# The mean row of the last three tiles as products with their rows, and the expert scores ahead of their transposes

## The chip, the cores and the metric

The kernel runs on one core of one Trainium2 chip. The time is what the device takes for one execution, in microseconds (us). The kernel before took 1511.21 us, the median of three runs (1510.18 to 1511.75).

## The reference, cut to what matters

A graph of 1250 nodes with 512 features passes two layers. In the first, `x` becomes the sum of `x`, a graph convolution and an attention block with its own MLP. Then comes the step that the change is about, a mixture of 16 experts that sees all nodes as one sequence and so chooses one expert for all of them:

```python
scores = softmax(mean(u, axis=1) @ Wg + bg, axis=-1)   # u: layer norm of x, 1 x 1250 x 512
idx    = argmax(scores, axis=-1)
gate   = take_along_axis(scores, idx[:, None], axis=-1)
y      = einsum('bsd,bdo->bso', u, We[idx]) + be[idx][:, None, :]
x      = x + gate[:, :, None] * y
```

So the mean of all 1250 normalized rows is needed before the index, and the index before any byte of the chosen expert's weights (512 x 512) is fetched. The second layer (another graph convolution, an attention and eight experts of 2048 hidden features, two per node) follows.

## The kernel before, in words

The 1250 rows are ten tiles (`T`) of 125 (`P`); features are four chunks (`DC`) of 128. `xs[:, t, :]` holds the rows of tile t, rows on partitions. The program is unrolled Python. A framework takes the order of the instructions on each engine from a simulated run: an instruction of a later line goes ahead of an earlier one on the same engine when its inputs are there first. Each engine then carries out its own list in that order, and semaphores hold an instruction until what it needs is done. TensorE, VectorE, ScalarE, GpSimd and SyncE (which issues most transfers) each have such a list.

The end of the first layer's MLP works in three blocks of tiles, `blocks = ((0, 4), (4, 7), (7, T))` (L697). For each block, `mlp_hidden` and `mlp_out` make the rows (L710, L722), and `expert_rows(b)` (L733) follows one block later, for the last block directly after its `mlp_out` (L779). `expert_rows` does, for its tiles:

- mean and variance of each row into `mvf` (`stats`, L143), then 1/std into `rstd` (`inv_std`, L135: an add on VectorE, a square root on ScalarE, a reciprocal on VectorE). In the last block, `load_table` (L749) has ScalarE load the table of Exp.
- for each tile: the normalized rows `un` (L743, VectorE; two buffers, tag "row"), four transposes on TensorE into one PSUM buffer `pt` (`transposed`, L128 to L133; two buffers), a copy of `pt` to `ut[t]` on ScalarE (L746), and the sum of `pt` over its 125 rows into `sums_t[:, t, :]` on VectorE (L747).

The next phase (from L831) opens its own pools. VectorE adds the ten parts of `sums_t` (L835) and multiplies by 1/N (L836). TensorE multiplies the mean with the router's weights into `psc`, 1 x 16 (L839). Then come, on VectorE but for the Exp on ScalarE: the bias (L841), the maximum (L843), the difference (L844), Exp (L845), the sum (L846), its reciprocal (L847), the quotient (L848), the largest value (L850) and its index `best_i` (L852). SyncE loads the index into a register (L853) and issues the four pieces of the chosen expert's weights `we_sb` (L856), the bias `be_sb` (L858) and, behind them, six weights of the second layer (L862). TensorE spreads the gate over the partitions (L871) and multiplies `ut` with `we_sb`, 40 products (L893): the first four tiles together, the others one by one. L877 sets `b2_full` to zero on VectorE, for a later use.

Two helpers of other places serve as rows of comparison: `degrees` (L573) has products with a moving operand of one column, and `project` (L123) in the second layer's router has them eight columns wide. L1306 and L1329 are the products of the eight experts at the end, and L1366, L1399 and L1400 their branches, since how many rows an expert gets is known only on the chip.

## Time and profile before

| what | value |
| --- | --- |
| median of three runs | 1511.21 us |
| the profiled execution, its own time | 1508.84 us |
| its span, from first to last instruction | 1507.1 us |
| mean granted clock of TensorE | 0.966 of full |
| stretch 505.0 to 525.0: TensorE, VectorE, ScalarE busy | 8.33, 12.27, 7.76 us |
| the same stretch: granted clock | 0.74 |
| stretch 525.0 to 562.5: TensorE, VectorE busy | 37.21, 28.20 us |
| the same stretch: granted clock | 0.91 |
| L747, sum of a transposed tile | ten of 0.674 us (median) |
| L132 for `un`, a transpose | 40 of 0.270 us (median) |
| L746, copy of a transposed tile | 0.53 us each |
| L852, index of the best expert, ends | 520.96 us |
| L856, first weight transfer issued | 522.39 us |
| L893, first product with the expert's weights | 525.29 us |

Times within the execution count from the start of the span. In lists in order of time, the first number is the start, the second the time over which the merged instructions reach, then the engine (PE is TensorE, PEld its weight loads, DVE VectorE, ACT ScalarE, SPq the transfers that SyncE issues), the line, the operation, output and inputs, how many; in brackets stands the idle time before and what ended it. Lines of the form `A:B` give, for the stretch from A to B: its length, TensorE's busy time (instructions), the granted clock as a share of full, the share of the transfer engines and GB/s. Where a line gives durations as a/b/c, they are the least, the median and the largest in ns.

### The profile page before, as it was taken

The page shows a single profiled execution, that of the slowest core. Times are in us where ns is not written, and L with a number is a line of the kernel's source. Part 1 is how long each engine was busy: PE and PEld are TensorE (multiplying, and loading weights), DVE is VectorE, ACT ScalarE, POOL GpSimd, SP SyncE. Part 2 cuts the span into 40 slices and gives each one's busy share as a digit, 9 for nine tenths or more (in the row PEclk, how much of TensorE's full clock was granted, in tenths as well). Part 3 has the DMA queues.
Part 4 walks back from the last instruction along what each step waited for, and adds up shares of the span by engine and source line. Part 5 has one row for each costly group of instructions (what it writes and reads, how often), then busy time and mean ns, then how long its engine had stood idle before and what let it go on. Part 6 is the DMA issues. An engine that isn't in the chain of part 4 may idle for free. (4 is left out here: it accounts for less than half of the span.)

```text
span 1507.1 us, 18469 instructions
## 1 busy us (share of the span) xinstructions
PE 1392.5 (92%) x6082; PEld 871.0 (58%) x6082; DVE 586.0 (39%) x1425; ACT 404.9 (27%) x937; POOL 199.3 (13%) x176
## 2 busy tenths in 40 slices
PE   5999999999999699999965899899999999999997
PEld 3444445434554346554544697794767577975673
DVE  8887777699775673344476000000000000000000
ACT  8655445301223413112223221210212012110110
POOL 3345445400000000000005000000000000000000
PEclk9999999999999899999986999899999999999999
DMA  7312111522510030001149466600643006101011
GB/s 225 99 55 62 56 55 49 178 83 89 172 48 14 31 131 3 0 1 36 47 152 349 149 222 236 227 9 11 230 125 115 13 3 215 36 6 14 1 14 15
DMA packets 72766, 134.75 MB, mean 89 GB/s; under 512 B 8328, under 2 KB 9720, under 8 KB 72622
## 3 DMA queue, kind: packets, MB, share of 16 engines
q1 hardware_dynamic: 67694, 122.47, 24.0%
q0 software_dynamic: 4928, 10.43, 3.5%
q8 instruction: 82, 1.34, 0.4%
q14 instruction: 62, 0.51, 0.1%
HBM read 107.27 MB, written 26.38 MB: 89 GB/s over the span
## 5 line engine op out<-in xcount | busy, mean ns | idle before, releaser
L1329 PE MATMUL po<-w,big 128*128 128x512 f32 x576 | 250.1, 592 | 0.0
L1306 PE MATMUL pm<-hts,big 128*128 x960 | 183.3, 353 | 14.8 <-issue 13.5
L1318 DVE TENSOR_SCALAR o<-po,to_gate 128x512 f32<-128x512 f32 (+1 forms) x24 | 17.7, 749 | 452.9 <-PE po L1331 451.6
L1306 PEld LDWEIGHTS pm<-hts,big 128*128 128x128 f32 x960 | 165.8, 194 | 34.4 <-issue 19.0
L1329 PEld LDWEIGHTS po<-w,big 128*128 128x128 f32 x576 | 109.1, 190 | 132.1 <-issue 131.5
L1309 ACT ACTIVATE big<-pm,cols_sb 128x256 f32<-128x256 f32 (+2 forms) x224 | 96.2, 433 | 282.5 <-PE pm L1306 281.8
L1306 PE MATMUL pm<-hts,w 128*128 x832 | 143.5, 334 | 13.8 <-PEq L1399 5.9
L1306 PEld LDWEIGHTS pm<-hts,w 128*128 128x128 f32 x832 | 132.1, 197 | 24.6 <-issue 15.6
L455 PE MATMUL pm<-big,ht 128*125 128x512 f32 x240 | 130.9, 633 | 0.0
L1319 POOL DMA_INDIRECT out_dram<-o,row x24 | 37.0, 1540 | 645.2 <-DVE o L1318 284.2
L429 DVE TENSOR_TENSOR at<-at,pa 128x160 f32 x320 | 102.2, 319 | 41.3 <-PE pa L427 17.7
L400 POOL TENSOR_TENSOR hm<-hm,w_low 125x640 bf16<-125x640 bf16 x80 | 100.4, 1276 | 114.0 <-DVE hm L394 63.3
L123 PE MATMUL pm<-w,at 128*125 128x512 f32 x240 | 114.2, 598 | 0.0
L397 ACT ACTIVATE hm<-hm,w_top 125x80 bf16<-125x80 bf16 x320 | 86.4, 350 | 68.1 <-DVE hm L394 55.1
L633 PE MATMUL pn<-big,at 125*125 125x512 f32 x200 | 89.5, 605 | 3.0 <-DMA big<-q_d 3.0
L455 PE MATMUL pm<-big,xt 128*125 128x512 f32 x160 | 88.8, 646 | 1.2 <-DMA x_t<-in_x_dram 1.2
L1309 ACT ACT_TABLE_LOAD x11 | 14.1, 1283 | 248.9 <-PE pm L1306 248.9
L427 PEld LDWEIGHTS <-hs 125*128 125x128 bf16 x640 | 50.8, 97 | 48.8 <-issue 44.0
L424 PE MATMUL pa<-hm,hs 125*128 125x160 bf16 x320 | 64.6, 233 | 13.0 <-DVE at L429 10.9
L424 PEld LDWEIGHTS <-hs 125*128 125x128 bf16 x320 | 31.1, 97 | 67.8 <-issue 38.6
L633 PEld LDWEIGHTS pn<-big,at 125*125 125x125 f32 x200 | 37.5, 190 | 52.7 <-issue 52.7
L427 PE MATMUL pa<-hm,hs 125*128 125x80 bf16 x640 | 64.4, 198 | 0.0
(391 smaller groups left out, 1622.2 us busy)
## 6 DMA issues: line engine op xcount, KB each, us to landing
w<-in_w_dram SPq DMA_DIRECT2D x52, 1024.0 KB
big<-in_w_dram SPq DMA_DIRECT2D x12, 1024.0 KB
x_t<-in_x_dram SPq DMA_DIRECT2D x10, 224.0 KB
xn_d<-xr SPq DMA_DIRECT2D x10, 224.0 KB
y_d<-o SPq DMA_DIRECT2D x10, 224.0 KB
z_d<-o SPq DMA_DIRECT2D x10, 224.0 KB
q_d<-o SPq DMA_DIRECT2D x10, 224.0 KB
k_d<-o SPq DMA_DIRECT2D x10, 224.0 KB
```

Source lines behind the costliest of these rows:

```text
L123: nc.tensor.matmul(ps, lhs[:, c, :], w[:, c, :], start=(c == 0), stop=(row is None and c == DC - 1))
L397: nc.scalar.activation(hm[:, j, 1, :], hm[:, j, 0, :], AF.Copy, scale=w_top[:, g * J + j:g * J + j + 1])
L400: nc.gpsimd.tensor_tensor(hm[:, :, 2 + i, :], hm[:, :, 0, :], w_low[:, i, c8, None].to_broadcast([CH, J, TW]), ALU.mult)
L424: nc.tensor.matmul(pa.rearrange("p k c -> p (k c)"), hs[:, j, :], hm[:, j, 0:2, :].rearrange("p k c -> p (k c)"), start=True, stop=False)
L427: nc.tensor.matmul(pa[:, 1, :], hs[:, j, :], hm[:, j, 2 + i, :], start=False, stop=(i == 1))
L429: add = nc.vector.tensor_tensor(to, to, pa.rearrange("p k (t w) -> p k t w", t=T), ALU.add)
L455: nc.tensor.matmul(pm, lhs[:, c, :], w_sb[:, c, :], start=(c == 0), stop=(row is None and c == DC - 1))
L633: nc.tensor.matmul(pn, at[:P, 0, s, t * P:(t + 1) * P], y[:, s, :], start=(s == 0), stop=(s == T - 1))
L1306: nc.tensor.matmul(pm[:, :width], w1s[e, f // DC][:, c, (f % DC) * 128:(f % DC + 1) * 128], hts[:, c, bass.ds(start, width)], start=(c == ...
L1309: nc.scalar.activation(hid[f][:, :width], pm[:, :width], AF.Gelu, bias=cols_sb[:, C_B11 + e * FC + f:C_B11 + e * FC + f + 1])
L1319: nc.gpsimd.indirect_dma_start(out, bass.IndirectOffsetOnAxis(ap=row[:n], axis=0), o[:n], None, bounds_check=N - 1, oob_is_err=False, comp ...
L1329: nc.tensor.matmul(pm, hid[f][:, s * 128:(s + 1) * 128], w2s[e, f // DC][:, f % DC, :], start=(f == 0), stop=False)
```

## The change

In the last block (tiles 7, 8 and 9) the sum of the normalized rows is no longer taken from the transposes. The sum over rows of (x - mean) * rstd is the product of x with the column rstd, less the product of the row means with rstd. So TensorE takes, per tile, each 128-feature chunk of `xs` as the stationary operand and `rstd` as a moving operand of one column; a fifth column of `pmean` has the row means, spread over 128 columns, as the stationary operand. That is fifteen products. VectorE adds the seven earlier tiles' parts ahead of the block's statistics, copies the fifth column out, and updates the mean's sum with the other four. The scaling by 1/N moves into the step that adds the bias. The scores' chain, up to the index, moves from the next phase into `expert_rows`, behind the transposes of tile 7 and the scaled rows of tile 8 and ahead of the rest of tiles 8 and 9. `mean_t`, the scalars and the scores use space of `sums_t` and `bg_sb`; `best` and `best_i` move to a pool that lasts longer. The other two blocks work as before.

```diff
+    mean_t, spare = sums_t[:, T - 1, :], sums_t[:, T - 2, :]
...
         def expert_rows(b):
             first, last = blocks[b]
+            final = b + 1 == len(blocks)
+            if final:
+                nc.vector.tensor_reduce(mean_t, sums_t[:, :first, :].rearrange("p t c -> p c t"), AX.X, ALU.add)
             for t in range(first, last):
                 stats(mvf, t, xs[:, t, :])
             rstd = inv_std(mvf[:, first:last, 1], [P, last - first], "rstd2")
-            if b + 1 == len(blocks):
+            if final:
                 load_table(AF.Exp, rstd[0:1, 0:1])
-            for t in range(first, last):
-                un = mx.tile([P, D], F32, name="un", tag="row")
-                nc.vector.tensor_scalar(un, xs[:, t, :], mvf[:, t, 0:1], rstd[:, t - first:t - first + 1],
+                pmean = pa.tile([128, DC + 1], F32, name="pmean", tag="pa")
+                for c in range(DC + 1):
+                    for t in range(first, last):
+                        lhs = (xs[:, t, c * 128:(c + 1) * 128] if c < DC else
+                               mvf[:, t, 0:1].to_broadcast([P, 128]))
+                        nc.tensor.matmul(pmean[:, c:c + 1], lhs, rstd[:, t - first:t - first + 1],
+                                         start=(t == first), stop=(t == last - 1))
+            uns = {}
+            def un_of(t):
+                uns[t] = mx.tile([P, D], F32, name="un", tag="row")
+                nc.vector.tensor_scalar(uns[t], xs[:, t, :], mvf[:, t, 0:1], rstd[:, t - first:t - first + 1],
                                         op0=ALU.subtract, op1=ALU.mult)
-                pt = transposed(ps, un)
+            def turned_of(t):
+                pt = transposed(ps, uns[t])
                 nc.scalar.copy(ut[t], pt)
-                nc.vector.tensor_reduce(sums_t[:, t, :], pt, AX.X, ALU.add)
+                return pt
+            if not final:
+                for t in range(first, last):
+                    un_of(t)
+                    nc.vector.tensor_reduce(sums_t[:, t, :], turned_of(t), AX.X, ALU.add)
+                return
+            un_of(first)
+            turned_of(first)
+            un_of(first + 1)
+            less, one, score = spare[:, 0:1], spare[0:1, 1:2], bg_sb
+            nc.vector.tensor_copy(less, pmean[:, DC:])
+            nc.vector.scalar_tensor_tensor(mean_t, pmean[:, :DC], less, mean_t, op0=ALU.subtract, op1=ALU.add)
+            psc = pa.tile([1, E0], F32, name="psc", tag="pa")
+            for c in range(DC):
+                nc.tensor.matmul(psc, mean_t[:, c:c + 1], wg_sb[:, c, :], start=(c == 0), stop=(c == DC - 1))
+            nc.vector.scalar_tensor_tensor(score, psc, 1.0 / N, bg_sb, op0=ALU.mult, op1=ALU.add)
...
+            nc.scalar.activation(score, score, AF.Exp)
...
+            nc.vector.max(best, score)
+            nc.vector.max_index(best_i, best, score)
+            turned_of(first + 1)
+            for t in range(first + 2, last):
+                un_of(t)
+                turned_of(t)
...
-        mean_t = fp.tile([128, DC], F32, name="mean_t")
-        nc.vector.tensor_reduce(mean_t, sums_t.rearrange("p t c -> p c t"), AX.X, ALU.add)
-        nc.vector.tensor_scalar(mean_t, mean_t, 1.0 / N, None, op0=ALU.mult)
-        psc = pa.tile([1, E0], F32, name="psc", tag="pa")
...
-        nc.vector.max_index(best_i, best, score)
         chosen = nc.sync.value_load(best_i[0:1, 0:1], min_val=0, max_val=E0 - 1)
```

The lines left out between the scores and the index are the same steps in the same order as before.

More of the change, by code (lines that the diff above doesn't have):

```diff
@@ L537, in gps_two_layer_kernel @@
     sums_t = keep.tile([128, T, DC], F32, name="sums_t")
+    mean_t, spare = sums_t[:, T - 1, :], sums_t[:, T - 2, :]
+    best = keep.tile([1, 8], F32, name="best")
+    best_i = keep.tile([1, 8], U32, name="best_i")
     spots = [(t, D) for t in range(4)] + [(6, D), (7, D), (8, 0), (9, 0), (0, 0), (1, 0)]
@@ new lines, in expert_rows @@
+            psc = pa.tile([1, E0], F32, name="psc", tag="pa")
+            for c in range(DC):
+                nc.tensor.matmul(psc, mean_t[:, c:c + 1], wg_sb[:, c, :], start=(c == 0), stop=(c == DC - 1))
+            nc.vector.scalar_tensor_tensor(score, psc, 1.0 / N, bg_sb, op0=ALU.mult, op1=ALU.add)
+            nc.vector.tensor_reduce(one, score, AX.X, ALU.max)
+            nc.vector.tensor_scalar(score, score, one, None, op0=ALU.subtract)
+            nc.scalar.activation(score, score, AF.Exp)
@@ L749, in load_table @@
+            nc.vector.tensor_reduce(one, score, AX.X, ALU.add)
+            nc.vector.reciprocal(one, one)
+            nc.vector.tensor_scalar(score, score, one, None, op0=ALU.mult)
+            nc.vector.max(best, score)
[4 more added lines that the diff above has]
+                turned_of(t)
         def load_table(func, behind):
@@ L833, in gps_two_layer_kernel @@
             tc.tile_pool(name="fpa", bufs=1, space=PSUM) as pa:
-        mean_t = fp.tile([128, DC], F32, name="mean_t")
-        nc.vector.tensor_reduce(mean_t, sums_t.rearrange("p t c -> p c t"), AX.X, ALU.add)
-        nc.vector.tensor_scalar(mean_t, mean_t, 1.0 / N, None, op0=ALU.mult)
-        psc = pa.tile([1, E0], F32, name="psc", tag="pa")
-        for c in range(DC):
-            nc.tensor.matmul(psc, mean_t[:, c:c + 1], wg_sb[:, c, :], start=(c == 0), stop=(c == DC - 1))
-        score = fp.tile([1, E0], F32, name="score")
-        nc.vector.tensor_add(score, psc, bg_sb)
-        one = fp.tile([1, 1], F32, name="one")
-        nc.vector.tensor_reduce(one, score, AX.X, ALU.max)
-        nc.vector.tensor_scalar(score, score, one, None, op0=ALU.subtract)
-        nc.scalar.activation(score, score, AF.Exp)
-        nc.vector.tensor_reduce(one, score, AX.X, ALU.add)
-        nc.vector.reciprocal(one, one)
-        nc.vector.tensor_scalar(score, score, one, None, op0=ALU.mult)
-        best = fp.tile([1, 8], F32, name="best")
-        nc.vector.max(best, score)
-        best_i = fp.tile([1, 8], U32, name="best_i")
-        nc.vector.max_index(best_i, best, score)
         chosen = nc.sync.value_load(best_i[0:1, 0:1], min_val=0, max_val=E0 - 1)
```

## The prediction

> **What bounds the kernel now.** I read the page first: TensorE is busy 92% of the span, and section 2 shows its digits at 9 almost everywhere but in slices 13 and 14 (about 505 to 525 us). The chain of waits reaches back only into the last experts, so for the changed place I read the list of instructions in order of time, then stretches with the granted clock.

> ```profile
> PE 1392.5 (92%) x6082; PEld 871.0 (58%) x6082; DVE 586.0 (39%) x1425; ACT 404.9 (27%) x937; POOL 199.3 (13%) x176
> ```

> ```profile
> 512.49 0.18 DVE L140 RECIPROCAL rstd<-rstd 125x3 f32<-125x3 f32 x1 [0.27 <-ACT rstd L139]
> 513.40 1.07 PE L132 MATMUL pt<-ident,un 125*128 125x125 f32 x8 [3.16 <-DVE un L743]
> 515.49 1.06 PE L132 MATMUL pt<-ident,un 125*128 125x125 f32 x4 [1.01 <-DVE sums_t L747]
> 516.72 0.48 DVE L877 MEMSET b_full<- 96x512 f32 x1 [0.80 <-PE pt L132]
> 517.20 0.68 DVE L747 TENSOR_REDUCE sums_t<-pt 128x4 f32<-128x500 f32 x1
> 517.91 0.22 DVE L835 TENSOR_REDUCE mean_t<-sums_t 128x4 f32<-128x40 f32 x1
> 518.51 0.27 PEld L839 LDWEIGHTS psc<-w,mean_t 128*1 128x1 f32 x8 [2.35 <-issue]
> 519.65 0.21 ACT L845 ACTIVATE score<-score 1x16 f32<-1x16 f32 x1 [2.48 <-DVE score L844]
> 525.29 0.50 PEld L893 LDWEIGHTS pm<-we_sb,at 128*125 128x125 f32 x2 [4.05 <-DMA we_sb<-in_we_dram]
> ```

> The reader is to see one serial chain in which TensorE mostly idles: 1/std of the last tiles (ready 512.67), transposes of tiles 7 and 8, of 9, the last sum, the mean, the scores at 518.51, Exp at 519.65, the index at 520.96 (from the same list), the expert's weights, and the first product with them at 525.29. From there TensorE is busy without a gap to 562, and later waits follow instructions that move along. So what this chain loses or gains passes on about 1:1. From 1/std to the first score product it takes 518.51 - 512.67 = 5.84 us; from the index to 525.29 it is 4.33 us of load, issue and transfer, which the change leaves alone.

> **The clock** is the second thing to see:

> ```profile
> 514.00:514.25 0.25, 0.25 (x5) 1.00 0.00 0
> 514.25:514.50 0.25, 0.22 (x3) 0.88 0.00 0
> 514.50:514.75 0.25, 0.00 (x0) 0.50 0.00 0
> ```

> ```profile
> 531.20:531.40 0.20, 0.20 (x1) 0.50 0.98 364
> 531.40:531.60 0.20, 0.20 (x2) 0.73 1.09 343
> 531.60:531.80 0.20, 0.20 (x2) 1.00 1.09 392
> ```

> It falls to 0.50 at 514.44 and comes back at 531.51. All other switches of this trace, read off quarter-us stretches, lie a multiple of 3.413 us from these. The stretch 511.03 to 514.44, before the fall, has TensorE busy 1.04 of 3.41 us.

> **What the change removes.** Three sums over transposed rows (L747, 0.67 us each), the total (0.22), the scaling (0.17). Of these only the last sum and what follows stood on the path; the sum of tile 7 also held tile 9's transposes until 515.49. The path loses all its 5.84 us and gets a new one.

> **What it adds to the path.** pmean is 5 columns x 3 tiles = 15 products. This kernel's fp32 products run as two instructions (L893: 40 products, x80), so 30 weight loads of 128 columns and 30 products of one column. The nearest row is the degrees' product, also one column wide:

> ```profile
> 359.48 2.32 PE L573 MATMUL pd<-ones,over_s 128*125 128x1 f32 x20
> ```

> One takes 0.25, so (2.32 - 0.25) / 19 = 0.109 us each at full clock: the whole weight is loaded for one column. At half clock the router's product is nearest:

> ```profile
> 778.12 0.38 PE L123 MATMUL pl<-wr_sb,at 128*125 128x8 f32 x1 [0.50 <-DVE at L163]
> ```

> ```profile
> 778.12 0.59 PE L123 MATMUL pl<-wr_sb,at 128*125 128x8 f32 x2 [0.50 <-DVE at L163]
> ```

> The second adds 0.21. They begin at about 512.72, as rstd is there.

> *If the clock holds*: 30 x 0.109 = 3.27, issue ends 515.99, result 0.14 later; the copy of the mean's column (0.16, as the gate's copy), the update (at most 0.22, as L835), about 0.2 us from start to start on VectorE, then 0.18 to TensorE as now (518.33 to 518.51): scores at 516.73. Gain 518.51 - 516.73 = 1.78.

> *If it falls at 514.44 as now*: 1.72 / 0.109 = 15.8 are done, 14.2 x 0.21 = 2.98, issue ends 517.42, result 517.6; the two VectorE steps let the scores start at 518.2, but tile 7's transposes stand before them on TensorE's queue (4 x 0.22 = 0.88, from 517.42), so 518.3. Gain 0.2. Were all 30 at half clock, they would end at 519.0 and the scores start near 519.9: a loss of 1.4.

> Whether one-column products count as activity is not in any row; those are the ends.

> [...] But here the clock fell after a window that was 31% busy, so I side with the row. [...]

> **Smaller terms.** The sum over the first seven tiles (0.2, nearest L835) becomes ready at 508.69, when VectorE has no gap until 511.8 (the residual add of the last tile starts 510.39, its product ends 510.24): cost 0.2. The scores' own VectorE steps are equal in number. Exp now shares ScalarE's queue with the copies of tiles 7 to 9 (0.53 each). If tile 8's copy is put ahead of Exp, it begins when its transposes end, about 1.0 us after the scores at half clock, and Exp starts 0.85 late (0.4 at full clock); if not, 0. If tile 8's transposes are placed ahead of the scores, where TensorE is free, scores are 0.5 to 0.9 late instead. The schedule does reorder: L877 ran in front of an earlier line's sum, and the degrees of the last line of the phase ran at 433. That memset, 0.48, may fall between scores as well, behind a wait for tile 9's transposes: 0 to 0.5.

> Behind the new wait on VectorE (the copy from pmean) stand the score steps and tile 9's scaled rows, which need tile 7's buffer; for them wait tile 9's transposes and copy. Cover: tile 7's result is first read after 56 of the 80 L893 instructions, near 552, and the next phase's PSUM banks are needed at 525, while the last copy ends near 521. Without the second cover, a late copy would move 525.29 one to one. No DMA is added; the four weight pieces, the bias and the later weights on SyncE's queue start with the index, as now.

> **Sum.** Clock falling: +0.2 - 0.2 - (0 to 0.9), middle -0.5 (slower). Clock holding: 1.78 - 0.2 - (0 to 0.5) = 1.1 to 1.6. Then the first L893 instructions come 0.855 us apart at half clock and 0.43 at full, so a half-clock stretch costs half its length: in this trace 6.2 us, 3.1 lost. A start before 525.2 may meet the edge at 528.10 instead of 531.51 (the 82% busy window up to 528.10 was not enough) and gain up to 1.7 more; a later start loses only half. The grid need not lie the same in other executions, so I keep the plain shift.

> The profiled execution took 1508.84 (span 1507.1 and 1.74 around it), 2.37 under the median 1511.21. I add the shift to the median: 1511.2 + 0.5 = **1511.7**.

> **What may outweigh it: code position.** 60 instructions come into TensorE's stream ahead of the experts' branches. The page's instruction queue moves 1.34 MB in 82 packets, 16.3 KB each; PE's waits before L1306 hold five stalls put to "issue", 19.2 us together, the longest 7.0, and one of 5.9 put to a branch (L1399); and branches differ:

> ```profile
> L1366 PEldq COMPARE_BRANCH x19: 65/195/4863, 856.8 to 1498.9; - x19
> ```

> A branch costs 0.07 to 4.9 us, so a shift of blocks may expose or hide one stall: -7.0 to +7.0 us, nearest the shorter ones, 3 to 4.

> [...]

> **Rivals.**
> - *A, forecast*: clock falls within the new products; 1510.8 to 1512.6. 0.27. For it: the fall at 514.44 with 31%.
> - *B*: the clock holds, 1.1 to 1.6 gained, up to 1.7 more by an earlier edge: 1508.0 to 1510.1, likeliest 1509.8. 0.20. For it: a window 50% busy at 463.24 did not fall.
> - *C, slower*: the code shift exposes one more branch stall in the experts, TensorE idle before L1306; decides from 3 us on; +3 to +7 on A: 1514.7 to 1518.7, likeliest 1515.2. 0.27. Against: many branches cost 0.07.
> - *D*: the shift hides a stall: -3 to -7: 1504.7 to 1508.7, likeliest 1508. 0.14.
> - *E*: the order isn't what the text says; tile 8's transposes run ahead of the scores at half clock: A + 0.4, 1512.1. 0.12.

> Within 0.2% (3.0 us, about what a measurement of this kernel can tell from no change) lie A, E, most of B and a little of C and D: 0.58. Faster: 0.12 of D and 0.05 of B, 0.17. Slower: 0.25 of C. For 8 in 10, I leave out the outer half of D and somewhat under half of C: **1506.5 to 1516.5**. The likeliest cases' own range is 1508.0 to 1512.6.

> **What will show it.** Thirty one-column products from about 512.7, 0.11 apart and then 0.21 if the clock falls; scores between 516.7 and 519.9 on the old scale; Exp behind a copy or not; the interval from index to first L893 still 4.3; PE's idle before L1306, stall by stall, against 19.2 + 5.9. If the products run elsewhere in the order, or the phases after 562 are reordered, I am wrong in kind.

## The result and the profile after

The changed kernel takes **1516.55 us** (median of 9 runs, 1515.59 to 1520.15); the kernel before, beside it, 1511.75 (9 runs, 1509.89 to 1514.32). The ratio is 1.0036, 95% interval 1.0024 to 1.0049: slower by 0.36%, 4.8 us between the medians. 1511.7 was predicted, with an upper end of 1516.5.

The profiled execution of after took 1515.95, its span is 1514.2, 7.1 us longer than before's 1507.1. First line of the page's part 1, which answers to the one shown of before:

```profile
PE 1403.0 (93%) x6112; PEld 880.4 (58%) x6112; DVE 583.7 (39%) x1423; ACT 404.6 (27%) x937; POOL 198.5 (13%) x176
```

TensorE has 30 more instructions, as the prediction counted, but 10.5 us more of busy time; 30 at 0.21 (half clock) would be 6.3. Something else runs slowly. The list in order of time, over the stretch that the prediction spoke of (up to L733 a line number is 3 higher than before: L576 is before's L573):

```profile
512.80 0.18 DVE L140 RECIPROCAL rstd<-rstd 125x3 f32<-125x3 f32 x1 [0.27 <-ACT rstd L139]
513.03 4.16 PE L755 MATMUL pmean<-rstd,big 125*128 125x1 f32 x24 [2.59 <-DVE rstd L140]
517.05 1.42 PE L755 MATMUL pmean<-rstd,mvf 125*128 125x1 f32 x6
518.34 1.70 PE L132 MATMUL pt<-ident,un 125*128 125x125 f32 x7
...
519.96 0.24 PEld L782 LDWEIGHTS psc<-w,sums_t 128*1 128x1 f32 x8 [0.32 <-issue]
...
520.53 4.20 PE L576 MATMUL pd<-ones,over_s 128*125 128x1 f32 x20
...
524.60 1.07 PE L132 MATMUL pt<-ident,un 125*128 125x125 f32 x4
524.77 0.17 DVE L578 COPY deg<-pd 125x10 f32<-125x10 f32 x1 [4.24 <-PE pd L576]
524.86 0.15 DVE L784 TENSOR_REDUCE sums_t<-bg_sb 1x1 f32<-1x16 f32 x1
...
525.29 0.21 ACT L786 ACTIVATE bg_sb<-bg_sb 1x16 f32<-1x16 f32 x1 [3.94 <-DVE bg_sb L785]
...
525.84 0.48 DVE L906 MEMSET b_full<- 96x512 f32 x1 [0.58 <-PE pt L132]
526.25 0.10 DVE L787 TENSOR_REDUCE sums_t<-bg_sb 1x1 f32<-1x16 f32 x1
...
532.03 1.19 PE L922 MATMUL pm<-we_sb,at 128*125 128x512 f32 x1 [4.34 <-DMA we_sb<-in_we_dram]
```

The reader is to see the new products, 24 and 6, from 513.03 on; seven transposes ahead of the scores (519.96); and then something that belongs to none of this: the ten products of `degrees(1)`, 20 instructions, 4.20 us, in the middle of the scores. VectorE's queue has their copy (L578) between the bias and the maximum (L784), so the maximum waits for them with the whole chain behind it. In the kernel before the same twenty instructions ran in pieces between 416 and 434 us (L573), the last six here:

```profile
433.46 0.71 PE L573 MATMUL pd<-ones,over_s 128*125 128x1 f32 x6
```

The list of waits puts a price on the new place; of after:

```profile
DVE deg L578 <- PE pd L576: 4.2, 1, 4.2
```

**Why there.** `pd` lies in the PSUM pool of two buffers, tag "pa". The change takes two tiles of this pool, `pmean` and `psc`, in lines that stand ahead of `degrees(1)` in the program. The buffers go round in the order of the text, so `pd` gets its buffer only when `pmean` has been read (518.9); before, neither stood ahead of it, and its last products ran 85 us earlier. That is a reading of program and trace; e1 and e2 below test it.

**Balance**, from the end of 1/std to the first product with the expert's weights: before 512.67 to 525.29, 12.62; after 512.98 to 532.03, 19.05. End against end, +6.74:

| part | before | after | more |
| --- | --- | --- | --- |
| 1/std ready | 512.67 | 512.98 | 0.31 |
| to the scores' first product | 5.84 | 6.98 | 1.14 |
| scores to Exp | 1.14 | 5.33 | 4.19 |
| Exp to the index | 1.31 | 1.97 | 0.66 |
| index to the first expert product | 4.33 | 4.77 | 0.44 |

The last experts' stalls stood still; of after, the list of waits over the whole span, and over the stretch from 569 to the end:

```profile
PE pm L1335 <- PEq L1428: 6.0, 1, 6.0
```

```profile
PE pm L1335 <- issue: 19.4, 5, 6.5
```

The same two of before:

```profile
PE pm L1306 <- PEq L1399: 5.9, 1, 5.9
```

```profile
PE pm L1306 <- issue: 19.2, 5, 7.0
```

The time from the first expert product to the full clock is 6.2 us in both. So 6.7 of the 7.1 us that the span grew by are in the five parts above.

### The profile page after: what moved, and what is told of

Same layout as the page of the kernel before. It is cut to its first block, busy times and chain, and to the rows that moved or that the text cites. A ratio compares the mean times of both kernels' runs of the same rounds, so it can differ in the third digit from the quotient of the medians.

```text
span 1514.2 us, 18523 instructions
## 1 busy us (share of the span) xinstructions
PE 1403.0 (93%) x6112; PEld 880.4 (58%) x6112; DVE 583.7 (39%) x1423; ACT 404.6 (27%) x937; POOL 198.5 (13%) x176
## 5 line engine op out<-in xcount | busy, mean ns | idle before, releaser
L1335 PEld LDWEIGHTS pm<-hts,w 128*128 128x128 f32 x832 | 133.0, 198 | 24.8 <-issue 15.8
L123 PE MATMUL pm<-w,at 128*125 128x512 f32 x240 | 114.3, 598 | 0.0
```

What stands on the lines that cost most here:

```text
L123: nc.tensor.matmul(ps, lhs[:, c, :], w[:, c, :], start=(c == 0), stop=(row is None and c == DC - 1))
L1335: nc.tensor.matmul(pm[:, :width], w1s[e, f // DC][:, c, (f % DC) * 128:(f % DC + 1) * 128], hts[:, c, bass.ds(start, width)], start=(c == ...
```

## The experiments

The **theory**: the place of the degrees costs some 4 us; the rest is products at half clock and things that slipped between the steps. **Rivals**: the products and the clock alone cost it all; or the branches of the experts do. In each profile I read the same chain. Its parts are the ones above (Exp taken into "scores to index", the last part split where SyncE issues the first weight transfer); "half clock" is the time from the first expert product to the full clock, of which half is lost (in before these products' weights are loaded every 0.855 us up to 531.42 and every 0.43 us from 531.89 on). The ratios are estimated from all runs and are not the quotients of the medians.

| kernel | to scores | to index | to issue | to product | sum | half clock | ratio to before, interval |
| --- | --- | --- | --- | --- | --- | --- | --- |
| before | 5.84 | 2.45 | 1.43 | 2.90 | 12.62 | 6.2 | 1 |
| after | 6.98 | 7.30 | 1.53 | 3.24 | 19.05 | 6.2 | 1.0036, 1.0024 to 1.0049 |
| e1, degrees first | 5.93 | 3.20 | 1.53 | 3.18 | 13.84 | 5.7 | 1.0015, 1.0004 to 1.0026 |
| e2, before, degrees late | 10.00 | 2.45 | 1.43 | 2.86 | 16.74 | 3.1 | 1.0030, 1.0019 to 1.0040 |
| e3, scores last | 7.54 | 2.99 | 1.53 | 3.25 | 15.31 | 6.1 | 1.0015, 1.0000 to 1.0030 |
| e5, wide products in the gap | 5.98 | 3.20 | 1.53 | 3.15 | 13.86 | 5.6 | 1.0012, 1.0001 to 1.0023 |
| e4, 1/std split | 6.22 | 2.74 | 1.54 | 3.27 | 13.77 | 4.0 | 1.0003, 0.9993 to 1.0014 |
| e6, order held | 5.87 | 2.37 | 1.86 | 3.18 | 13.28 | 5.6 | 1.0004, 0.9995 to 1.0013 |
| e7, last tile alone | 4.84 | 2.37 | 1.86 | 3.16 | 12.23 | 5.9 | 0.9990, 0.9980 to 1.0000 |
| e9, before, zeroing late | 5.87 | 2.46 | 1.42 | 2.77 | 12.52 | 5.8 | 0.9998, 0.9988 to 1.0008 |
| e8, sums first | 4.28 | 2.37 | 1.54 | 3.12 | 11.31 | 3.4 | 0.9984, 0.9971 to 0.9998 |
| e10, before, sums first | 5.26 | 2.51 | 1.45 | 2.85 | 12.07 | 6.2 | 0.9998, 0.9983 to 1.0012 |

In every row the chain's difference to before lies inside the interval of the time, so the chain accounts for the times as far as they can be told apart. One part of it is luck. In the profiles of before and after every switch of the clock lies a multiple of 3.413 us from every other; in those of e1, e2, e3 and e5 the fall and the rise around this chain lie 5, 5, 6 and 5 times 3.413 us apart. Counted from the start of the span, this grid begins at 2.4 us in before, 2.3 in after, 3.1 in e1, 1.8 in e2, 1.0 in e3 and 2.8 in e5, so it lies differently against the program in these executions. In after the fall came 1.3 us behind the start of the new products, in e1 2.4, in e3 0.9; the half-clock column differs for the same reason.

### e1: degrees(1) ahead of the last block's rows

```diff
+        degrees(1)
         expert_rows(len(blocks) - 1)
-        degrees(1)
```

> The change with one line moved: the second call of the degrees stands ahead of the last block's expert rows, so that its PSUM tile comes before pmean and psc in their pool of two. Theory T (the degrees' ten products were pushed from 433 us into the middle of the scores, where VectorE stood behind them for 4.2 us): they go back to about 433, from 1/std to the first expert product 19.0 - 4.4 = 14.6 us, and the time falls by 4 to 5 to about 1512.2. Rival R (the fifteen new products and their half clock are the whole cost): at most 1 less, 1515.5 or more. Rival C (stalls at the experts' branches moved): no change, 1516.5.

1510.95 against 1509.18. The degrees are back at 418 to 436 us, and scores to index fell from 7.30 to 3.20. In the list in order of time:

```profile
516.12 3.10 PE L755 MATMUL pmean<-rstd,big 125*128 125x1 f32 x24 [2.59 <-DVE rstd L140]
...
521.99 0.24 PEld L782 LDWEIGHTS psc<-w,sums_t 128*1 128x1 f32 x8 [0.32 <-issue]
...
523.27 0.21 ACT L786 ACTIVATE bg_sb<-bg_sb 1x16 f32<-1x16 f32 x1
523.76 0.48 DVE L906 MEMSET b_full<- 96x512 f32 x1 [0.76 <-PE pt L132]
524.17 0.10 DVE L787 TENSOR_REDUCE sums_t<-bg_sb 1x1 f32<-1x16 f32 x1
```

One line of the program moved took 5.2 us from the chain, out of the 6.4 that the change had added. 4.1 of it, scores to index, is the place of the degrees; 1.05 is the grid's luck, since the products end 4.44 us from 1/std here and 5.49 in after, and from their end to the scores it is 1.49 in both. The theory expected a chain of 14.6 and 4 to 5 us of time; between the ratios it is 0.21%, 3.2 us. What is left, 1.2 us, is the zeroing (L906), which waits for tile 9's transposes between Exp and the sum behind it, and 0.4 behind the index; 1/std to scores is as long as before. With this fall of the clock, the products neither gain nor lose.

### e2: the kernel before, with only the degrees made late

```diff
                 pt = transposed(ps, un)
+                if t == T - 1:
+                    for i in range(2):
+                        hold = pa.tile([1, 1], F32, name="hold", tag="pa")
+                        nc.tensor.matmul(hold, un[:, 0:1], un[:, 0:1], start=True, stop=True)
```

Two products of one element take both buffers of the pool, at tile 9, as `pmean` and `psc` do.

> The kernel before with the degrees' second part alone made late: two products of one element, with tile 9's scaled rows, take both PSUM buffers of the pool, so the degrees come behind them. Nothing of the change is in it. T: twenty products' instructions at about half clock, 4.4 us, stand ahead of tile 9's transposes, so +3.5 to +4.5 on the kernel before: 1515.5. R: nothing that matters, within 1 of the kernel before (1511 to 1512.7).

1512.93 against 1509.18. In its list in order of time:

```profile
516.40 0.24 PE L751 MATMUL hold<-un 125*1 125x1 f32 x4 [0.18 <-DVE un L743]
516.65 3.86 PE L573 MATMUL pd<-ones,over_s 128*125 128x1 f32 x20
520.55 0.17 DVE L575 COPY deg<-pd 125x10 f32<-125x10 f32 x1 [4.20 <-PE pd L573]
520.63 1.25 DVE L747 TENSOR_REDUCE sums_t<-pt 128x4 f32<-128x500 f32 x2
```

Here too the products come as soon as the pool lets them, at half clock from 517.21 on, and the copy of `deg` makes VectorE wait 4.20 us with two sums behind it. The chain grows by 4.1 us and the time by 0.30% (about 4.5 us; 3.5 to 4.5 were expected), with none of the change's products in the program. So the buffers' turn alone is enough for most of the loss, and neither the clock of the new products nor the branches are needed for it.

### e3 and e5: the order of the scores, and the clock

Both stand on e1. In e3 the scores' chain stands behind all transposes in the text; in e5 three products of 512 columns, whose result nobody reads, stand ahead of `pmean`.

```diff
 e5
+                wide = ps.tile([P, D], F32, name="pm")
+                for i in range(3):
+                    nc.tensor.matmul(wide, xs[:, first + 1, :P], xs[:, first + 1, :], start=(i == 0), stop=(i == 2))
```

> e1 with the scores' chain written behind all transposes of tiles 8 and 9, as the part 'mean by products' alone. T: the order of the text matters little, since tile 8's transposes run ahead of the scores anyhow: 0.2 to 1.0 above e1, 1512.4 to 1513.2. If 'scores ahead' is what saves, 1.5 or more above e1.

> e1 plus three useless products, 125 by 512, of tile 8's rows, in TensorE's gap of 2.6 us before the new products (their result is not read). If the half clock makes the fifteen products long (5.4 us in place of 3.3): the clock stays full over them, they take 3.3 to 3.6, and the time is 1.5 to 2.2 below e1, about 1510.3. If one-column products take as long at full clock here, or the gap isn't what lets the clock fall: the time of e1 or up to 0.5 more.

e3 took 1513.36, e5 1511.21, beside 1509.18. e3 loses 1.6 us of chain to scores against e1. 1.41 of it lies ahead of the products' end (5.85 us from 1/std in place of 4.44), since the clock fell 0.9 us from 1/std, where in e1 2.5 us had gone by; 0.20 lies behind it (1.69 for 1.49), where eight transposes run ahead of the scores in place of seven. So the scores' place in the text is worth 0.2, at the low end of what the theory gave it, and the ratio is that of e1. e5 closes TensorE's gap ahead of the products, which was to keep the clock up. Its stretches, cut at the clock's grid (columns: length; busy time and instructions of PE, PEld, DVE, ACT and POOL; granted clock; share of the transfer engines; GB/s):

```profile
511.41:514.82 3.41, 3.41 (x9) 1.44 (x8) 3.41 (x9) 0.00 (x0) 0.00 (x0) 1.00 0.00 0
514.82:518.23 3.41, 3.39 (x24) 2.55 (x23) 1.66 (x6) 1.69 (x3) 0.00 (x0) 1.00 0.02 5
518.23:521.64 3.41, 3.41 (x18) 3.25 (x17) 0.73 (x3) 0.36 (x1) 0.00 (x0) 0.50 0.00 0
```

The second window was busy for 3.39 of 3.41 us, its first 1.04 with wide products and the rest with one-column ones, and the clock still fell at its end. So it falls without the gap too, and the scores came no sooner than in e1.

### e4: 1/std in two parts

1/std of tiles 7 and 8 is made ahead of tile 9's, and the products go tile by tile.

```diff
-            rstd = inv_std(mvf[:, first:last, 1], [P, last - first], "rstd2")
+                for lo, hi in ((first, last - 1), (last - 1, last)):
...
-                for c in range(DC + 1):
-                    for t in range(first, last):
+                for t in range(first, last):
+                    for c in range(DC + 1):
```

> As the version with the degrees first (1510.95 in its run, 0.15% over the kernel before), but 1/std of the last block is made in two parts, tiles 7 and 8, then tile 9, and the products go tile by tile. The theory (the place of the degrees cost 4 us; what is left is the products at half clock, 3.0 to 4.5 us from 1/std) expects the 20 instructions of tiles 7 and 8 ahead of the last 1/std, so that some 10 are left behind it: 10 x 0.22 = 2.2 instead of 4.5, against one more set of three small steps ahead of it (add, root, reciprocal, near 0.6): scores from 1 to 2 us sooner, ratio to the kernel before 1.0000 to 1.0010. The rival (the products themselves are not what is late; it is the clock edge or the load of the weights) expects no change against the version with the degrees first: 1.0015.

1509.76 against 1508.50, inside the theory's range for the time, but its reason failed: the scores came 6.22 us behind the last 1/std, no sooner than in e1. The first part was there only 0.65 us ahead of the second, so some 6 instructions (at 0.109) and not 20 went ahead, and the clock fell 1.3 us behind the first of them. In its profile the full clock is back after 4.0 us instead of e1's 5.7, which is worth 0.9 of time there. This run tells nothing for or against the theory.

### e6 and e7: order held; the last tile alone by products

e6 is e1 with tile 8's and 9's transposes held behind the scores' products, their copies behind Exp, tile 9's scaled rows and the zeroing behind the index. e7 keeps this and takes only tile 9's part by products; tiles 7 and 8 are summed from the transposes, as before.

```diff
 e6
+            with tc.issue_after(held["psc"]), tc.issue_after(held["exp"]), tc.issue_after(held["index"]):
+                turned_of(first + 1)
+                for t in range(first + 2, last):
+                    un_of(t)
+                    turned_of(t)
...
+        m = nc.vector.memset(b2_full, 0.0).ins
+        tc.add_manual_dep(m, indexed.name, NO_SYNC, reason="the index goes first")
 e7
-                    for t in range(first, last):
+                    for t in range(last - 1, last):
...
+            for t in (first, first + 1):
+                nc.vector.tensor_reduce(sums_t[:, t, :], turned_of(t), AX.X, ALU.add)
```

> The version with the degrees first, with the order held to that of the text: the transposes of tiles 8 and 9 behind the score products, their copies behind Exp, tile 9's scaled rows and the zeroing of the bias tile behind the index. The theory expects from the score products to the index 2.45 us as in the kernel before (3.20 with the degrees first alone, where the zeroing stood between Exp and the sum), and the score products 0.3 to 0.7 us sooner since no transposes run ahead of them: 0.8 to 1.4 us under the version with the degrees first, ratio to the kernel before 1.0005 to 1.0010. The rival (what stands between the steps is hidden anyway, the copies behind the index are late for the experts instead) expects 1.0015 or more, with a new wait of TensorE before the first experts.

> Degrees first and order held as in the one before, but only tile 9's part comes by products with its rows, 5 of them in place of 15; tiles 7 and 8 are summed from their transposes as in the kernel before. The theory (30 half-clock instructions are dearer than one tile's transposes and sum) expects 1/std to the score products in 3.9 to 4.5 us instead of the 5.84 of the kernel before and the 5.93 with all three tiles by products, and the index 2.45 us behind: 1.0 to 2.0 us faster than the kernel before, ratio 0.9987 to 0.9993. The rival (the sums of tiles 7 and 8 on VectorE, 0.7 us each, end later than the products, so they set the time) expects 1/std to the scores in 5.5 us or more and a ratio of 1.000 or above.

e6: 1509.31, e7: 1507.69, before 1508.50. Scores to index is 2.37 in both: with the zeroing, and all else that stood between the steps, behind the index, the 0.8 us of e1 are gone. e6's scores come only 0.06 sooner than e1's (0.3 to 0.7 expected): from the end of the products to the scores it takes 0.86 (517.72 to 518.58) in place of 1.49, with three transposes fewer in front, but the products themselves end 5.01 from 1/std in place of 4.44, since the clock fell earlier in them (24 took 3.68, in e1 3.10). So e6 has 0.56 us less chain than e1, where 0.8 to 1.4 less were expected. e7 needs 4.84, more than the 3.9 to 4.5 expected: each sum waits for ScalarE's copy of the same tile. Its ratio lies in the range expected, its chain, 0.39 us under before, does not. And both pay 0.43 between index and issue. Of e7, in order of time:

```profile
514.45 0.58 ACT L764 COPY at<-pt 128x500 f32<-128x500 f32 x1 [1.10 <-PE pt L132]
515.06 0.68 DVE L780 TENSOR_REDUCE sums_t<-pt 128x4 f32<-128x500 f32 x1 [1.13 <-ACT at L764]
...
516.88 0.24 PEld L784 LDWEIGHTS psc<-w,mean_t 128*1 128x1 f32 x8 [2.03 <-DVE mean_t L781]
...
519.84 1.07 PE L132 MATMUL pt<-ident,un 125*128 125x125 f32 x4 [2.59 <-DVE un L759]
...
521.11 2.02 SPq L888 DMA_DIRECT2D we_sb<-in_we_dram  x4
```

Tile 9's transposes end at 520.91, and 0.20 later the transfer is issued; in e6 it is 522.61 and 522.81. The weights' tile seems to wait until they have read their rows. That is a reading of two equal gaps; e8 tests it.

### e8 and e9 and e10: what the order is worth without the products, and with them

e9 is the kernel before with the zeroing behind the index, nothing else. e8 is e7 with the sums ahead of the copies and a free buffer (tag "in") for tile 9's scaled rows, so that its transposes follow the scores' products. e10 does the same to e9: no products for the mean at all.

```diff
 e8
-                uns[t] = mx.tile([P, D], F32, name="un", tag="row")
+                uns[t] = mx.tile([P, D], F32, name="un", tag="row" if t < T - 1 else "in")
...
-                nc.vector.tensor_reduce(sums_t[:, t, :], turned_of(t), AX.X, ALU.add)
+                pt = transposed(ps, uns[t])
+                nc.vector.tensor_reduce(sums_t[:, t, :], pt, AX.X, ALU.add)
+                nc.scalar.copy(ut[t], pt)
```

> The kernel before with nothing else changed than the zeroing of the bias tile (0.48 us on VectorE, ahead of the sum of tile 9) held behind the index. The theory that this chain passes on one to one expects the score products 0.3 to 0.5 us sooner and a time 0.3 to 0.5 us (0.03%) under the kernel before, less than the timing tells and to be read from the trace; the rival (the sum waits for tile 9's transposes, which end when the zeroing does) expects the score products at the same distance from 1/std, 5.84 us.

> The version with the last tile alone by products (index to 1/std 7.2 us, 1/std to scores 4.84), with two more things: the sums of tiles 7 and 8 stand ahead of ScalarE's copies of the same tiles (there each sum waited 0.6 us for the copy), and tile 9's scaled rows take a free buffer, so that its transposes stand right behind the score products and not behind the index (there the load of the expert's weights was issued 0.20 us behind these transposes, 1.86 us from the index in place of 1.43). If the chain from 1/std to the first expert product is what counts, 1/std to the scores takes 4.2 to 4.4 us, index to issue 1.4 to 1.55, and the whole chain 11.2 to 11.6 where the kernel before has 12.62: 1.0 to 1.5 us faster than it, ratio 0.9988 to 0.9994. If sums and copies only change places and the load waits for something else, nothing against the version with the last tile alone by products, 12.2.

> The kernel before without any product for the mean: only the sums of the last block put ahead of ScalarE's copies, the zeroing of the bias tile behind the index, and a free buffer for tile 9's scaled rows. It asks whether the products are needed at all. If the order is most of it, 1/std to the scores falls from 5.84 to 4.8 to 5.2 us and the time by 0.6 to 1.0 us, ratio 0.9993 to 0.9997; what is left between this and the version with tile 9 by products (0.5 to 0.9 us) is what the products are worth. If the sums wait for the transposes anyway, 5.5 us or more and no gain.

e9: 1508.27 against 1508.50, and scores 5.87 from 1/std. The rival was right: the sum waits for tile 9's transposes and copy, so the zeroing cost nothing where it was.

e8: 1510.29 against 1512.75, ratio 0.9984. Its chain hit all three numbers (4.28, 1.54, 11.31). In order of time:

```profile
517.84 0.68 DVE L782 TENSOR_REDUCE sums_t<-pt 128x4 f32<-128x500 f32 x1 [0.78 <-PE pt L132]
...
518.56 0.58 ACT L783 COPY at<-pt 128x500 f32<-128x500 f32 x1 [1.88 <-DVE sums_t L782]
...
519.66 0.24 PEld L787 LDWEIGHTS psc<-w,mean_t 128*1 128x1 f32 x8 [1.42 <-DVE mean_t L784]
...
519.97 1.10 PE L132 MATMUL pt<-ident,un 125*128 125x125 f32 x4
...
523.57 2.02 SPq L889 DMA_DIRECT2D we_sb<-in_we_dram  x4
```

The copy now waits for the sum, off the chain, and with tile 9's transposes at 519.97 the issue stands 1.54 from the index again, which fits the reading above. 1.3 us of the gain are chain; 1.4 more, in this execution alone, is the full clock, back after 3.4 us where before has 6.2: luck with the grid, as in e2, which starts its expert products late and has 3.1. The ratio is better than the 0.9988 to 0.9994 expected, whose range lies within its interval. e10, without products, has 5.26 (4.8 to 5.2 expected) and 12.07, by 0.55 shorter than before, and 1513.09 against 1512.75: no change that can be measured. So of e8's 1.3 us of chain, the order alone gives 0.55; the other 0.76 come with the five products for the last tile and the scores in the earlier phase, which no run takes apart. By its interval (0.02% to 0.29%) **e8 is a little faster than the kernel before**, where the change is slower.

## Why the prediction was wrong

- **What bounds it, and that this chain passes on one to one**: right in the profiled pair, +6.74 at the chain's end and +7.1 of span; by the ratio's interval the time grew by 3.6 to 7.4. e2 shows the same for the old kernel.
- **The products' price and the clock**: right. 0.11 us each held at full clock, 0.21 at half. The clock fell at 514.29, inside the products, as forecast A had it. The gain of 1.78 us needed the full clock over all the products. Here the gap ahead of them was 2.6 us (the wait in their row), the window up to the fall was busy for 1.25 of 3.41 us, all of it one-column products, and the clock fell. In e5, with the gap filled, it fell behind a window busy for 3.39 of 3.41 us, 1.04 of it wide products. What makes it fall was not shown.
- **1/std later**: 0.31 for the 0.2 forecast, but 0.21 of it had come about by the end of the block's last MLP product (510.45 for 510.24). From there to 1/std it is 2.53 for 2.43; the added sum cost 0.1.
- **Order around the scores**: three of tile 8's transposes ran ahead of them, as in rival E: 0.63, by 1.49 from the products' end to the scores here and 0.86 in e6. The products' end came 5.49 from 1/std (518.47), where A's sum has 4.9: the clock fell 1.3 us into them, not 1.7. So 1/std to scores took 6.98, and the forecast's 5.6 and up to 0.9 more end at 6.5. ScalarE's copies last 0.58 us each (L746, median of ten), not the 0.53 given for them above; tile 8's ran ahead of Exp, at 520.77, and delayed nothing, since Exp waited for the degrees.
- **The zeroing between the scores, 0 to 0.5**: it fell there and cost up to 0.66 (Exp to index), 0.83 by e1 against e6, somewhat more than allowed.
- **The step that failed**: "The scores' own VectorE steps are equal in number", with which scores to index was left at its 2.45. It took 7.30. Equal steps don't make an equal chain when another line's step comes between them on the queue. The text named the degrees as a row of prices, and even as a line that ran far ahead of its place, at 433; it didn't ask what let them run so early, nor what pool `pmean` and `psc` were taken from. The queues that the moved steps pass were counted, the buffers that they take were not. 4.19 of the 4.85 us lie between the scores and Exp, where the degrees' copy stands, and e1 took 4.1 of them back. The price could have been had from the prediction's own rows: 20 instructions at 0.21, 4.2 us, and 1511.7 + 4.2 = 1515.9.
- **Index to the first product, "left alone"**: 4.77 for 4.33. 0.10 of it is the issue, 0.34 the transfer's start. It shows in all eight kernels in which the scores stand in the earlier phase (3.12 to 3.27 from issue to product) and in none of the four others (2.77 to 2.90). The cause stays open: in these eight one packet of instructions (0.01 MB) goes over another queue, q14, just ahead of the data, in the four others none, but no run took it away.
- **Code position, rival C**: the time fell into its range by chance, not by its mechanism. The stalls were 19.4 and 6.0 for 19.2 and 5.9. The 3 to 7 us of rivals C and D, and with them the ends of the forecast's range, rest on the author's estimate that the added instructions, by a shift of blocks of instructions, expose or hide a stall; no run shows that.

## What to carry to other kernels

In these kernels a tile taken in a line that moves up goes round its pool in the order of the text: the products of `degrees(1)` ran at 416 to 434 us in before, at 520.53 behind `pmean` in after, at 516.65 behind `hold` in e2, and at 418 to 436 again in e1. Before pricing a move, list every later tile of the same pool: whoever used that buffer early, for free, now runs behind the moved step, and can land on the queues in front of what follows. Here a step that had run 85 us earlier landed on the critical chain by one such turn.

Where two engines read one PSUM tile, the one that stood second in the text waited in e7 and e8 (e7: copy to 515.03, sum from 515.06; e8: sum to 518.52, copy from 518.56). So the one that the chain waits for should stand first: that and a free buffer for tile 9's rows shortened this chain by 0.55 us in e10, too little to be seen in its time.

## What the hardware showed that I had not expected

```profile
510.88:514.29 3.41, 1.25 (x12) 1.26 (x12) 2.76 (x9) 1.69 (x3) 0.00 (x0) 1.00 0.00 0
514.29:517.70 3.41, 3.41 (x19) 3.41 (x18) 0.00 (x0) 0.00 (x0) 0.00 (x0) 0.50 0.02 5
517.70:521.12 3.42, 3.42 (x24) 3.04 (x24) 1.09 (x4) 0.92 (x2) 0.00 (x0) 0.50 0.00 0
521.12:524.53 3.41, 3.41 (x18) 3.41 (x18) 0.00 (x0) 0.23 (x1) 0.00 (x0) 0.50 0.00 0
...
534.77:538.19 3.42, 3.42 (x6) 1.33 (x5) 0.20 (x1) 0.00 (x0) 0.00 (x0) 0.50 0.98 292
538.19:541.60 3.41, 3.41 (x9) 1.48 (x8) 3.41 (x6) 0.00 (x0) 0.00 (x0) 1.00 1.05 390
```

In the first window TensorE has nothing but products for the mean, 1.25 us of them, and the clock falls at its end. The second window is full of them, the third of transposes, scores and the first degrees, the fourth of nothing but degrees; none raised the clock. The window from 534.77 is full of products of 512 columns, and behind it the clock is up. It need not be quite full: a window that such products kept busy for 2.81 us did not raise the clock in before, one with 3.12 us did in e2:

```profile
524.69:528.10 3.41, 2.81 (x4) 1.25 (x5) 0.00 (x0) 0.00 (x0) 0.00 (x0) 0.50 0.91 291
530.87:534.28 3.41, 3.12 (x4) 1.48 (x5) 0.00 (x0) 0.00 (x0) 0.00 (x0) 0.50 0.87 259
```

So in these profiles the clock, once down, stayed at half through a window of nothing but one-column products, 3.41 us of them, and was up again behind windows that products of 512 columns had kept busy for 3.12 us in e2 and 3.42 in after. The fall itself came 1.3 us into the products in after and, with the gap filled, 2.4 us into them in e5. How much a one-column product counts, if anything, no run settles.
